# First layer of a two-layer graph network: two edge tiles in one 128 by 384 product, tables of two partial sums, x kept in DRAM

## The chip, the cores and the metric

The kernel runs on one core of a Trainium2 chip. The metric is the device time of one execution in microseconds; the time of a kernel is the median of its runs. A core has five engines that run side by side, each with its own queue of instructions: TensorE (PE; its weight loads are shown as PEld), VectorE (DVE), ScalarE (ACT), GpSimd (POOL) and SyncE (SP), which here issues DMAs. Gathers by index (indirect DMAs) are issued by POOL.

## The reference

12500 nodes with 64 features; 212500 edges, sorted by target node, of which 12500 are self-loops. Each edge has a source, a target, a type out of 16 and 8 attributes.

```python
h = jnp.maximum(_layernorm(x, axis=-1), 0.0)
# layer 0: per edge, the row of its source times the weight of its type; summed by target
for r in range(num_rels):
    mask = etypes == r
    msg = msg + h_src * mask[:, None].astype(feat.dtype) @ weight[r]
x = x + segment_sum(msg, dst)
h = jnp.maximum(_layernorm(x, axis=-1), 0.0)
# layer 1: a small network per edge on (source row, target row, attributes); summed by target
z = jax.nn.relu(concat([h[src], h[dst], edge_attr]) @ W1 + b1)
x = x + segment_sum(z @ W2 + b2, dst)
```

## The kernel before, in words

**Tiles and groups.** Nodes are taken in 98 blocks of 128 rows. The 200000 edges that are not loops are compacted into 1563 tiles of 128 edges, and a group is G = 4 tiles. Since edges are sorted by target, the targets of a tile lie within a window of WT = 12 nodes. The first layer takes the 392 groups of loopless edges (line 1005), the second layer 416 groups of all edges (line 1098).

**The first layer.** For each group POOL gathers the normalised source rows, 128 rows of 64 values per indirect DMA, one per tile (`gather`, line 737), into one of 14 row buffers (`land`, line 303); the first eight groups are gathered from x itself into buffers of their own (32 gathers, `gather_raw`, line 351) and normalised afterwards. ACT makes a one-hot of 16 types by 12 window places for each edge (`relations`, line 750): four ACTIVATEs for the distances and one for the one-hot. PE multiplies, per tile, the rows (128 edges by 64 features) with the one-hot (128 edges by 192) in two halves of HW = 96 columns (`products`, line 983): even types come out on partitions 0 to 63, odd types on 64 to 127. DVE adds the 128 by 96 result into a table at the window of the tile (`add`, line 993). Two tables alternate, each with 8 rows (RH) of 384 nodes: a block pair of 256 nodes and AHEAD = 128 nodes of the next.

**Closing a step.** A step is two blocks, about eight groups. When its groups are added (FIN1, line 139), ACT copies the head of the next step's nodes into the other table (`go_on`, line 771), and `finish` (line 776) folds the table: four pairs of products with `wrel` (line 786), summed in PSUM, then a transposing product; DVE adds the block of x, which lies in SBUF for the whole run (`x_sb`, line 218); then the norm and the projections of the second layer, stored to `a_rows`, `a_early` and `b_rows` by SP. `begin` (line 852) starts the table two steps ahead with the self-loops: PE turns the rows, DVE writes eight rows of the table (line 880).

**What sets the order.** Each engine's instructions are kept in the order in which they are written (`InOrder`, line 316). The work of a step is cut into small pieces by `yield`, and one or more pieces of `open_step` (finish), `fresh` (begin) and `coming` (preparing later edges: compaction, codes, loops) are taken after each add (lines 1048 to 1051). In iteration `it` POOL gathers group it + 8, ACT makes its one-hot, PE multiplies group it + 6 (`L1_PE`, lag 2) and DVE adds group it + 3 (`L1_ADD`, lag 5); near the end the lags shrink to 1 and 2. Products wait in four PSUM buffers of one group (line 1039). The compaction's results are scattered to DRAM by indirect DMAs on POOL, between the gathers (`store`, line 534).

**The second layer.** POOL gathers `a_rows` by source; the first four groups (EARLY) read `a_early`, which misses the last two blocks, and the rest read `a_rows`, after its last store. SP fetches a window of `b_rows` per group (line 1116). PE, DVE and ACT make the hidden rows, PE sums them by target, DVE adds to `sums`; `results` (line 1069) multiplies by W2, adds x from `x_sb` and stores the output.

Of the kernel before, what the change touches and what calls it, by code (L numbers as in the profile page):

```python
# [50 lines left out]
P = 128  # L51
# [20 lines left out]
G = 4  # L72
# [4 lines left out]
HW = RH * WT  # L77
# [31 lines left out]
L1_PE, L1_ADD = (2, 1), (5, 2)  # L109
# [84 lines left out]
def gnn_kernel(  # L194
# [11 lines left out]
    b_rows = dram.tile([NW, D], F32, name="b_rows")  # L206
    dst_l = dram.tile([NGR, G * P], BF16, name="dst_l")
# [10 lines left out]
    x_sb = keep.tile([P, NB * D], F32, name="x_sb")  # L218
    x3 = x_sb.rearrange("p (b d) -> p b d", d=D)
    tail = N - (NB - 1) * P  # L220

    def load_x(b0, Q):

        full = min(b0 + LB, NB - 1)
        Q.dma_start(x3[:, b0:full, :], x[b0 * P : full * P].rearrange("(b p) d -> p b d", p=P))
        if b0 + LB == NB:
            V.memset(x3[:, NB - 1, :], 0.0)
            Q.dma_start(x3[:tail, NB - 1, :], x[(NB - 1) * P :])
# [26 lines left out]
    def layer_norm(pool, b0, nb, name):  # L255

        shape = [P, nb, D]
        mv, rs = stats(pool, x3[:, b0 : b0 + nb, :], nb, name)
        h = pool.tile(shape, F32, name=f"{name}_h")
        V.tensor_tensor(h, x3[:, b0 : b0 + nb, :], bc(mv[:, :, 0], 2, D, shape), op=ALU.subtract)  # L260
        V.scalar_tensor_tensor(h, h, 0.0, bc(rs, 2, D, shape), op0=ALU.max, op1=ALU.mult)
        return h
# [37 lines left out]
    def in_order():  # L300
        with ExitStack() as c2:
# [63 lines left out]
            tables = [own.tile([P, RH, SN + AHEAD], F32, name=f"table{k}") for k in range(2)]  # L365
# [3 lines left out]
            G_.iota(rsel, pattern=[[2, RH]], base=0, channel_multiplier=0, allow_small_or_imprecise_dtypes=True)  # L369
            V.tensor_single_scalar(rsel[D:], rsel[D:], 1.0, op=ALU.add)  # L370
# [12 lines left out]
            wrel = own.tile([P, RH, D], F32, name="wrel")  # L383
# [24 lines left out]
            def weights():  # L408
                for k in range(2):
                    Q_.dma_start(wrel[k * D : (k + 1) * D], w_rel[k::2].rearrange("r i o -> i r o"))  # L410
# [136 lines left out]

            def codes_raw():

                f = prep.tile([P, RAWT], I32, name="raw_f", bufs=1)  # L550
                row = prep.tile([1, RAWT], I32, name="raw_r", bufs=1)
                even = prep.tile([P, RAWT], I32, name="raw_e", bufs=1)
                rel = prep.tile([P, RAWT], I32, name="raw_t", bufs=1)
                d = prep.tile([P, RAWT], F32, name="raw_d", bufs=1)
                ok = prep.tile([P, RAWT], F32, name="raw_ok", bufs=1)
                bad = prep.tile([P, RAWT], F32, name="raw_bad", bufs=1)
                Q_.dma_start(f, raw_f.unsqueeze(0).to_broadcast([P, RAWT]))
                Q_.dma_start(row, raw_f.unsqueeze(0))
# [3 lines left out]
                V_.tensor_single_scalar(even, rel, 1, op=ALU.bitwise_and)  # L562
# [3 lines left out]
                V_.scalar_tensor_tensor(ok, rel, float(R), ok, op0=ALU.is_le, op1=ALU.mult)  # L566
                yield
                V_.tensor_tensor(d, dst_r, f, op=ALU.subtract)
                V_.scalar_tensor_tensor(bad, d, float(WT), d, op0=ALU.is_ge, op1=ALU.mult, accum_out=next(odds_of))
                V_.scalar_tensor_tensor(d, rel, float(WT // 2), d, op0=ALU.mult, op1=ALU.add)  # L570
                yield
                V_.scalar_tensor_tensor(d, even, -float(HW - WT // 2), d, op0=ALU.mult, op1=ALU.add)
                V_.scalar_tensor_tensor(d, d, float(1 + HW - WT), ok, op0=ALU.add, op1=ALU.mult)
# [97 lines left out]
            def codes(c, q, row, psA, V, S, T, rest):  # L671
# [20 lines left out]
                V.tensor_single_scalar(even, rel, 1, op=ALU.bitwise_and)  # L692
                yield
                V.tensor_tensor(d, q[:n, :, :, 1], bc(first_d, 2, P, [n, 2, P]), op=ALU.subtract)
# [5 lines left out]
                V.scalar_tensor_tensor(d, rel, float(WT // 2), d, op0=ALU.mult, op1=ALU.add)  # L700
                V.scalar_tensor_tensor(d, even, -float(HW - WT // 2), d, op0=ALU.mult, op1=ALU.add)
                yield
                V.tensor_single_scalar(ok, rel, 1.0, op=ALU.is_ge)
                V.scalar_tensor_tensor(ok, rel, float(R), ok, op0=ALU.is_le, op1=ALU.mult)
# [4 lines left out]
                V.scalar_tensor_tensor(d, d, float(1 + HW - WT), ok, op0=ALU.add, op1=ALU.mult)  # L709
# [66 lines left out]
            def finish(k, psA):  # L776
# [3 lines left out]
                long = nb == BS  # L780
                if long:
                    yield from rest(2)
# [3 lines left out]
                for r in range(0, RH, 2):  # L786
                    for k in range(2):
# [5 lines left out]
                            stop=(r + 2 == RH),  # L793
                        )
                    if long:
                        yield from rest(2)
# [7 lines left out]
                x_b = x3[:, b0 : b0 + nb, :]  # L804
                V_.tensor_tensor(x_b, x_b, pT[:, :nb, :], op=ALU.add)
                st = wk.tile([P, nb, 6], F32, name="s_st")
# [3 lines left out]
                for i in range(nb):  # L810
                    V_.bn_stats(st[:, i, :], x3[:, b0 + i, :])
# [46 lines left out]
            def some(t, at, b0, n, psA):  # L858
# [20 lines left out]
                yield from rest(2)  # L879
                for r in range(RH):  # L880
# [79 lines left out]
            def first_layer(psA, loops_0):  # L960
# [22 lines left out]
                def products(g, i):  # L983
                    for half in range(2):
                        T_.matmul(
                            pa_of[g][half * D : (half + 1) * D, i, :],
                            lhsT=rows_of[g][:, i, :],
                            rhs=oh_of[g][:, i, half * HW : (half + 1) * HW],
                            start=True,
                            stop=True,  # L990
                        )

                def add(a, i):
                    k = a * G + i
                    if i < n_of[a]:
# [5 lines left out]
                        to = tables[STEP1[a] % 2][:, :, bass.ds(at.pop(k), WT)]  # L1001
                        V_.tensor_tensor(to, to, pa_of[a][:, i, :].rearrange("p (r n) -> p r n", r=RH), op=ALU.add)

                at = {}
                for it in range(NG1 - RAWG + L1_ADD[1]):
                    g = it + RAWG
                    if g < NG1:
# [6 lines left out]
                        if it % 56 == 4 and it // 56 < NB // LB:  # L1014
                            load_x(it // 56 * LB, Q_)
# [21 lines left out]
                    for g in now:  # L1037

                        pa_of[g] = psA.tile([P, G, HW], F32, name="pa", bufs=4)
# [28 lines left out]

            def results(k, ps):
                (b0, nb), t = BLOCKS[k], sums[k % 2]  # L1070
                po = ps.tile([P, BS, D], F32, name="po", bufs=1)
# [5 lines left out]
                V_.tensor_tensor(o[:, :nb, :], po[:, :nb, :], x3[:, b0 : b0 + nb, :], op=ALU.add)  # L1077
# [12 lines left out]
            def second_layer(ps):  # L1090
# [6 lines left out]
                of_z, of_hid, of_pe, of_add = (turns(lag, NGR) for lag in (L2_Z, L2_HID, L2_PE, L2_ADD))  # L1097
                for it in range(NGR + L2_ADD[1]):
# [119 lines left out]
    def in_any_order():  # L1218
        for b0 in range(0, NB, XB):
            load_x(b0, nc.sync)  # L1220
        with ExitStack() as c0:
            rel_rows = dram.tile([NB * P, R * D], F32, name="rel_rows")
# [8 lines left out]
            with ExitStack() as c1:  # L1231
# [114 lines left out]
                def relation_products(b):  # L1346
                    if b % LB == 0:
                        hs[b // LB] = layer_norm(wk, b, LB, "r")
# [163 lines left out]
            with ExitStack() as c3:  # L1512
# [3 lines left out]
                for b0 in range(0, NB, LB):  # L1516
                    h = layer_norm(wk, b0, LB, "s")
# [165 lines left out]
```

## Time and profile before

| | us |
|---|---|
| median of 3 runs | 4092.42 |
| lowest and highest run | 4087.24, 4093.86 |
| the profiled execution | 4087.75 |
| its span, first to last instruction | 4085.9 |
| POOL busy in the span | 3083.5 |
| PE busy | 2422.0 |
| ACT busy | 1640.5 |
| DVE busy | 1146.0 |

A busy time counts the time in which at least one instruction of the engine runs. A line of a group gives the line of the code (here mostly the helper at line 325, so that tiles are told apart by name), the engine, the operation, the tiles written and read, shapes and number; then busy time, mean duration in ns, and the idle time before these instructions with what ended it. "issue" is idle time in which the engine waited for nothing that the profile shows. A line of the order of time begins with the start and the duration in us. The granted clock of PE is given in tenths of full speed.

The gathers from x start at 5.64 us, those from `h_rows` run from 50.9 us to 2002 us, and the second layer's from 2002.35 us to 4075.

### The profile page before, as it was taken

Reading aid. Unit: us, or ns where it says so; the run is one execution under the profiler, and the core shown is the slowest. Engines: PE = TensorE matmul, PEld = TensorE weight load, DVE = VectorE, ACT = ScalarE, POOL = GpSimd, SP = SyncE. Lnnn points to the kernel's source line nnn. Section 1 sums busy time; section 2 is a strip of 40 time slices with the busy share of each in tenths; the row PEclk is TensorE's granted clock in tenths of the full one; section 3 lists DMA queues with packets and bytes.
Section 4 is the critical chain, followed back from the end, with each engine's and each line's share of the span. In section 5 each row is a group of like instructions: output and inputs, shape, how many; then the busy total and the mean of one; then the engine's idle time right before and its main releaser. Section 6 shows DMA issues by size and latency. Waiting matters only on the chain. (4 is left out here: it accounts for less than half of the span.)

```text
span 4085.9 us, 49975 instructions
## 1 busy us (share of the span) xinstructions
PE 2422.0 (59%) x14840; PEld 1853.3 (45%) x14840; DVE 1146.0 (28%) x4671; ACT 1640.5 (40%) x3222; POOL 3083.5 (75%) x3274
## 2 busy tenths in 40 slices
PE   1655655555555555556686666666666666666655
PEld 0433333333333333333475555555555555555555
DVE  7533334333333333333211111111111111111111
ACT  6754545454545454545333222322232222322222
POOL 7777777777777777777777777777777777777776
PEclk9655555555555555555555555555555555555555
DMA  4222222121222222121222121111111112111111
GB/s 124 48 44 64 42 48 44 40 46 40 51 40 45 42 45 42 38 41 37 48 46 42 42 42 44 42 42 42 42 42 42 42 41 44 41 42 42 42 39 36
DMA packets 233554, 184.50 MB, mean 45 GB/s; under 512 B 162969, under 2 KB 171680, under 8 KB 232336
## 3 DMA queue, kind: packets, MB, share of 16 engines
q0 software_dynamic: 104320, 107.70, 14.1%
q1 hardware_dynamic: 115655, 70.30, 6.5%
q10 hardware_dynamic: 13298, 3.20, 0.4%
q8 instruction: 121, 1.98, 0.2%
q14 instruction: 160, 1.31, 0.1%
HBM read 162.74 MB, written 18.20 MB: 44 GB/s over the span
## 5 line engine op out<-in xcount | busy, mean ns | idle before, releaser
L325 POOL DMA_INDIRECT rows<-a_rows,src_i x1645 | 1552.2, 944 | 501.4 <-issue 428.9
L325 POOL DMA_INDIRECT rows<-h_rows,src_c x1535 | 1456.9, 949 | 468.2 <-issue 390.4
L325 PE MATMUL pa<-oh_r,rows 128*64 128x96 f32 x6140 | 836.2, 381 | 780.8 <-DMA rows<-h_rows,src_c 701.9
L325 PE MATMUL pz<-b_win,of_edges 48*128 48x64 f32 x3322 | 819.0, 424 | 686.3 <-ACT of_edges L325 682.1
L325 PEld LDWEIGHTS pz<-b_win,of_edges 48*128 48x128 f32 x3322 | 739.3, 324 | 735.7 <-ACT of_edges L325 712.0
L325 PEld LDWEIGHTS pa<-oh_r,rows 128*64 128x64 f32 x6140 | 472.4, 204 | 1193.8 <-DMA rows<-h_rows,src_c 848.8
L325 ACT ACTIVATE hid<-z 128x256 f32<-128x256 f32 x416 | 172.9, 416 | 1429.7 <-DVE z L325 1399.3
L325 DVE TENSOR_TENSOR z<-pz,rows 128x256 f32<-128x256 f32 x416 | 176.3, 424 | 1652.4 <-DMA rows<-a_rows,src_i 1520.3
L325 ACT ACTIVATE off_r<-iota_s,code 128x192 bf16<-128x192 f32 x1535 | 568.1, 441 | 0.0
L325 DVE TENSOR_TENSOR table<-table,pa 128x96 f32 x1567 | 395.6, 252 | 368.6 <-PE pa L325 262.1
L325 PE MATMUL pa<-oh,hid 128*65 128x40 f32 x3322 | 456.8, 312 | 38.3 <-ACT hid L325 27.2
L325 PEld LDWEIGHTS pa<-oh,hid 128*65 128x65 f32 x3322 | 395.9, 226 | 88.6 <-ACT hid L325 30.8
L325 ACT ACTIVATE oh_r<-off_r 128x768 f32<-128x768 bf16 x392 | 330.2, 842 | 211.5 <-PE pa L325 203.6
L325 DVE SCALAR_TENSOR_TENSOR table<-b_rel,rsel,hT 128x256 f32<-128x256 f32 (+1 forms) x400 | 171.6, 467 | 401.8 <-PE hT L325 391.6
L325 ACT ACTIVATE off<-local_bc,neg_w 40x1024 bf16<-40x1024 bf16 x208 | 235.8, 1134 | 21.5 <-DMA local_bc<-dst_l 12.9
L325 ACT ACTIVATE of_edges<-off 40x1024 f32<-40x1024 bf16 x208 | 219.7, 1056 | 6.5
L325 PE MATMUL pT<-table,wrel 128*64 128x256 f32 (+1 forms) x800 | 200.0, 596 | 2.1 <-DVE table L325 2.1
L325 DVE TENSOR_TENSOR oh<-local,iota_p 128x160 f32<-128x160 f32 x416 | 128.5, 310 | 0.0
L325 DVE TENSOR_TENSOR x_sb<-x_sb,pT 128x128 f32<-128x128 f32 (+1 forms) x50 | 14.2, 284 | 394.5 <-PE pT L325 394.5
L325 ACT COPY table<-table 128x1024 f32<-128x1024 f32 x49 | 51.2, 1045 | 143.0 <-DVE table L325 143.0
L325 ACT ACTIVATE s_rs<-s_mv,eps 128x2 f32<-128x2 f32 (+1 forms) x50 | 14.8, 296 | 230.9 <-DVE s_mv L325 230.9
L325 DVE TENSOR_TENSOR sums<-sums,pa 65x40 f32 x416 | 75.2, 181 | 46.1 <-PE pa L325 33.8
(193 smaller groups left out, 1049.6 us busy)
## 6 DMA issues: line engine op xcount, KB each, us to landing
rows<-a_rows,src_i POOLq DMA_INDIRECT x1645
rows<-h_rows,src_c POOLq DMA_INDIRECT x1535
local_bc<-dst_l SPq DMA_DIRECT2D x104, 160.0 KB
of_edges<-in_attr_t SPq DMA_DIRECT2D x104, 64.0 KB
b_win<-b_rows SPq DMA_DIRECT2D x416, 10.0 KB
b_rel<-t_loop SPq DMA_DIRECT2D x48, 128.0 KB
l_in<-in_rows_l SPq DMA_DIRECT2D x4, 1009.5 KB
b_h<-h_rows SPq DMA_DIRECT2D x48, 64.0 KB
```

Source lines behind the costliest of these rows:

```text
L325: last_ins[self.engine] = getattr(self.engine, name)(*args, **kw)
```

## The change

Two tiles share one product. The rows of tiles i and i + 1 (128 edges by 2 x 64) are multiplied with the one-hots of both (128 edges by 2 x 192). Of the 128 by 384 result the two diagonal blocks are wanted: tile i on partitions 0 to 63, tile i + 1 on partitions 64 to 127. Each is added, 64 partitions by 192, to its half of the table. The table now has 16 rows of types on both halves, and each half is a partial sum; on the lower half types are turned by 8 (`turned_by`), so that the self-loops, which `begin` writes, still need only eight rows, and ACT zeroes the other eight. Folding takes 8 pairs of products instead of 4, and the head copy is twice as wide. PSUM holds two groups instead of four, and the adds follow at lag 3 instead of 5. To make room in SBUF, x isn't kept there: `finish` loads its block of x from DRAM and stores the sum to `x_mid`, and `results` reads that back, loaded two steps ahead.

```diff
-L1_PE, L1_ADD = (2, 1), (5, 2)
+L1_PE, L1_ADD = (2, 1), (3, 2)
...
+    x_mid = dram.tile([NB * P, D], F32, name="x_mid")
...
-    x_sb = keep.tile([P, NB * D], F32, name="x_sb")
...
-            tables = [own.tile([P, RH, SN + AHEAD], F32, name=f"table{k}") for k in range(2)]
+            tables = [own.tile([P, R, SN + AHEAD], F32, name=f"table{k}") for k in range(2)]
...
-            wrel = own.tile([P, RH, D], F32, name="wrel")
+            wrel = own.tile([P, R, D], F32, name="wrel")
+            nought = own.tile([P, 1], F32, name="nought")
...
+            def turned_by(rel, past, V):
+
+                V.tensor_scalar(past, rel, float(RH + 1), -float(R), op0=ALU.is_ge, op1=ALU.mult)
+                V.scalar_tensor_tensor(rel, past, float(RH), rel, op0=ALU.add, op1=ALU.add)
...
+                x_b = wk.tile([P, BS, D], F32, name="x_b", bufs=2)[:, :nb]
...
+                    Q_.dma_start(x_b, x[rows].rearrange("(b p) d -> p b d", p=P))
                 if long:
                     yield from rest(2)
...
-                for r in range(0, RH, 2):
+                for r in range(0, R, 2):
...
                     if long:
-                        yield from rest(2)
+                        yield
...
                 V_.tensor_tensor(x_b, x_b, pT[:, :nb, :], op=ALU.add)
+                Q_.dma_start(x_mid[rows, :].rearrange("(b p) d -> p b d", p=P), x_b)
...
+                for r in range(RH, R, 4):
+                    S_.copy(t[:, r : r + 4, at : at + n * P], bc(nought.to_broadcast([P, n * P]), 1, 4, [P, 4, n * P]))
+                    yield
                 for r in range(RH):
...
                 def products(g, i):
-                    for half in range(2):
-                        T_.matmul(
-                            pa_of[g][half * D : (half + 1) * D, i, :],
-                            lhsT=rows_of[g][:, i, :],
-                            rhs=oh_of[g][:, i, half * HW : (half + 1) * HW],
-                            start=True,
-                            stop=True,
-                        )
+                    if i % 2:
+                        return
+                    n = min(2, n_of[g] - i)
+                    T_.matmul(
+                        pa_of[g][: n * D, i // 2, : n * RW],
+                        lhsT=rows_of[g][:, i : i + n, :].rearrange("p i d -> p (i d)"),
+                        rhs=oh_of[g][:, i : i + n, :].rearrange("p i c -> p (i c)"),
+                        start=True,
+                        stop=True,
+                    )
...
-                        to = tables[STEP1[a] % 2][:, :, bass.ds(at.pop(k), WT)]
-                        V_.tensor_tensor(to, to, pa_of[a][:, i, :].rearrange("p (r n) -> p r n", r=RH), op=ALU.add)
+                        half = slice(i % 2 * D, i % 2 * D + D)
+                        to = tables[STEP1[a] % 2][half, :, bass.ds(at.pop(k), WT)]
+                        V_.tensor_tensor(to, to, pa_of[a][half, i // 2, i % 2 * RW :][:, :RW].rearrange("p (r n) -> p r n", r=R), op=ALU.add)
...
-                        if it % 56 == 4 and it // 56 < NB // LB:
-                            load_x(it // 56 * LB, Q_)
...
-                        pa_of[g] = psA.tile([P, G, HW], F32, name="pa", bufs=4)
+                        pa_of[g] = psA.tile([P, G // 2, 512], F32, name="pa", bufs=2)
...
+            def load_mid(k):
+                b0, nb = BLOCKS[k]
+                mids[k] = wk2.tile([P, BS, D], F32, name="x_r", bufs=3)[:, :nb]
+                Q_.dma_start(mids[k], x_mid[b0 * P : (b0 + nb) * P, :].rearrange("(b p) d -> p b d", p=P))
...
-                V_.tensor_tensor(o[:, :nb, :], po[:, :nb, :], x3[:, b0 : b0 + nb, :], op=ALU.add)
+                V_.tensor_tensor(o[:, :nb, :], po[:, :nb, :], mids.pop(k), op=ALU.add)
```

The path for edges in any order (not taken on these inputs) gets its own copy of x in SBUF.

More of the change, by code (lines that the diff above doesn't have):

```diff
@@ L76 @@
 RH = R // 2
-HW = RH * WT
 AHEAD = 128
@@ L217, in gnn_kernel @@
     V.memset(eps, EPS)
-    x_sb = keep.tile([P, NB * D], F32, name="x_sb")
-    x3 = x_sb.rearrange("p (b d) -> p b d", d=D)
     tail = N - (NB - 1) * P
[L222 to L228, printed above, removed]
     flag = keep.tile([1, 1], I32, name="flag")
@@ L253, in stats, with layer_norm @@
         return mv, rs[:, 1, :]
-    def layer_norm(pool, b0, nb, name):
+    def layer_norm(pool, x3, b0, nb, name):
         shape = [P, nb, D]
@@ L364, in in_order @@
             xf = load_front(fr)
-            tables = [own.tile([P, RH, SN + AHEAD], F32, name=f"table{k}") for k in range(2)]
+            tables = [own.tile([P, R, SN + AHEAD], F32, name=f"table{k}") for k in range(2)]
             src_c = own.tile([P, UPTO[-1]], I32, name="src_c")
             rsel = own.tile([P, RH], F32, name="rsel")
-            G_.iota(rsel, pattern=[[2, RH]], base=0, channel_multiplier=0, allow_small_or_imprecise_dtypes=True)
-            V.tensor_single_scalar(rsel[D:], rsel[D:], 1.0, op=ALU.add)
+            G_.iota(rsel, pattern=[[1, RH]], base=0, channel_multiplier=0, allow_small_or_imprecise_dtypes=True)
+            V.tensor_single_scalar(rsel[D:], rsel[D:], float(RH), op=ALU.add)
             place_c = own.tile([P // 2, PARTS, 2], F32, name="place_c")
@@ L382, in in_order @@
             G_.memset(none, -1.0)
-            wrel = own.tile([P, RH, D], F32, name="wrel")
+            wrel = own.tile([P, R, D], F32, name="wrel")
+            nought = own.tile([P, 1], F32, name="nought")
+            V.memset(nought, 0.0)
             local = own.tile([P, NT], F32, name="local")
@@ L409, in weights @@
                 for k in range(2):
-                    Q_.dma_start(wrel[k * D : (k + 1) * D], w_rel[k::2].rearrange("r i o -> i r o"))
+                    Q_.dma_start(wrel[k * D : (k + 1) * D, :RH], w_rel[k * RH :][:RH].rearrange("r i o -> i r o"))
+                    Q_.dma_start(wrel[k * D : (k + 1) * D, RH:], w_rel[RH - k * RH :][:RH].rearrange("r i o -> i r o"))
                     Q_.dma_start(w1ab[k * D : (k + 1) * D], w1[: 2 * D].rearrange("(k i) o -> i k o", k=2))
@@ L561, in codes_raw @@
                 V_.tensor_single_scalar(rel, rel, float(R + 1), op=ALU.min)
-                V_.tensor_single_scalar(even, rel, 1, op=ALU.bitwise_and)
                 yield
@@ L566, in codes_raw @@
                 V_.scalar_tensor_tensor(ok, rel, float(R), ok, op0=ALU.is_le, op1=ALU.mult)
+                turned_by(rel[:, 1::2], even[:, 1::2], V_)
                 yield
@@ L569, in codes_raw @@
                 V_.scalar_tensor_tensor(bad, d, float(WT), d, op0=ALU.is_ge, op1=ALU.mult, accum_out=next(odds_of))
-                V_.scalar_tensor_tensor(d, rel, float(WT // 2), d, op0=ALU.mult, op1=ALU.add)
+                V_.scalar_tensor_tensor(d, rel, float(WT), d, op0=ALU.mult, op1=ALU.add)
                 yield
-                V_.scalar_tensor_tensor(d, even, -float(HW - WT // 2), d, op0=ALU.mult, op1=ALU.add)
-                V_.scalar_tensor_tensor(d, d, float(1 + HW - WT), ok, op0=ALU.add, op1=ALU.mult)
+                V_.scalar_tensor_tensor(d, d, float(1 - WT), ok, op0=ALU.add, op1=ALU.mult)
                 V_.tensor_scalar(raw_code, d, -1.0, 1.0, op0=ALU.mult, op1=ALU.add)
@@ L691, in codes @@
                 V.tensor_single_scalar(sf, low, float(N - 1), op=ALU.min)
-                V.tensor_single_scalar(even, rel, 1, op=ALU.bitwise_and)
+                V.tensor_single_scalar(ok, rel, 1.0, op=ALU.is_ge)
+                V.scalar_tensor_tensor(ok, rel, float(R), ok, op0=ALU.is_le, op1=ALU.mult)
                 yield
+                turned_by(rel[:, 1], even[:, 1], V)
                 V.tensor_tensor(d, q[:n, :, :, 1], bc(first_d, 2, P, [n, 2, P]), op=ALU.subtract)
@@ L697, in codes @@
                 yield
[L700 to L704, printed above, removed]
+                V.scalar_tensor_tensor(d, rel, float(WT), d, op0=ALU.mult, op1=ALU.add)
                 yield
@@ L708, in codes @@
                     V.scalar_tensor_tensor(ok, place_w, float(RAWE), ok, op0=ALU.is_ge, op1=ALU.mult)
-                V.scalar_tensor_tensor(d, d, float(1 + HW - WT), ok, op0=ALU.add, op1=ALU.mult)
+                V.scalar_tensor_tensor(d, d, float(1 - WT), ok, op0=ALU.add, op1=ALU.mult)
                 V.tensor_scalar(d, d, -1.0, 1.0, op0=ALU.mult, op1=ALU.add)
@@ L780, in finish @@
                 long = nb == BS
+                x_b = wk.tile([P, BS, D], F32, name="x_b", bufs=2)[:, :nb]
+                rows = slice(b0 * P, (b0 + nb) * P)
+                if b0 == NB - 1:
+                    V_.memset(x_b, 0.0)
+                    Q_.dma_start(x_b[:tail, 0], x[b0 * P :])
+                else:
+                    Q_.dma_start(x_b, x[rows].rearrange("(b p) d -> p b d", p=P))
                 if long:
@@ L792, in finish @@
                             start=(r == 0),
-                            stop=(r + 2 == RH),
+                            stop=(r + 2 == R),
                         )
                     if long:
-                        yield from rest(2)
+                        yield
                 yield from rest(2)
@@ L803, in finish @@
                 yield from rest(2)
-                x_b = x3[:, b0 : b0 + nb, :]
                 V_.tensor_tensor(x_b, x_b, pT[:, :nb, :], op=ALU.add)
+                Q_.dma_start(x_mid[rows, :].rearrange("(b p) d -> p b d", p=P), x_b)
                 st = wk.tile([P, nb, 6], F32, name="s_st")
@@ L810, in finish @@
                 for i in range(nb):
-                    V_.bn_stats(st[:, i, :], x3[:, b0 + i, :])
+                    V_.bn_stats(st[:, i, :], x_b[:, i, :])
                 for i in range(nb):
@@ L1066, in first_layer @@
                     pass
+            mids = {}
+            def load_mid(k):
+                b0, nb = BLOCKS[k]
+                mids[k] = wk2.tile([P, BS, D], F32, name="x_r", bufs=3)[:, :nb]
+                Q_.dma_start(mids[k], x_mid[b0 * P : (b0 + nb) * P, :].rearrange("(b p) d -> p b d", p=P))
             def results(k, ps):
                 (b0, nb), t = BLOCKS[k], sums[k % 2]
+                if k + 2 < NFIN:
+                    load_mid(k + 2)
                 po = ps.tile([P, BS, D], F32, name="po", bufs=1)
@@ L1097, in second_layer @@
                 of_z, of_hid, of_pe, of_add = (turns(lag, NGR) for lag in (L2_Z, L2_HID, L2_PE, L2_ADD))
+                for k in range(2):
+                    load_mid(k)
                 for it in range(NGR + L2_ADD[1]):
@@ L1218, in in_any_order @@
     def in_any_order():
-        for b0 in range(0, NB, XB):
-            load_x(b0, nc.sync)
         with ExitStack() as c0:
+            x_sb = c0.enter_context(tc.tile_pool(name="x", bufs=1)).tile([P, NB * D], F32, name="x_sb")
+            x3 = x_sb.rearrange("p (b d) -> p b d", d=D)
+            for b0 in range(0, NB, XB):
+                full = min(b0 + XB, NB - 1)
+                nc.sync.dma_start(x3[:, b0:full, :], x[b0 * P : full * P].rearrange("(b p) d -> p b d", p=P))
+            V.memset(x3[:, NB - 1, :], 0.0)
+            nc.sync.dma_start(x3[:tail, NB - 1, :], x[(NB - 1) * P :])
             rel_rows = dram.tile([NB * P, R * D], F32, name="rel_rows")
@@ L1347, in relation_products @@
                     if b % LB == 0:
-                        hs[b // LB] = layer_norm(wk, b, LB, "r")
+                        hs[b // LB] = layer_norm(wk, x3, b, LB, "r")
                     h = hs[b // LB]
@@ L1516, in in_any_order @@
                 for b0 in range(0, NB, LB):
-                    h = layer_norm(wk, b0, LB, "s")
+                    h = layer_norm(wk, x3, b0, LB, "s")
                     a_st = wk.tile([P, LB, D], F32, name="a_st")
```

## Prediction

> **What bounds the kernel now.** I read the head of the page first, then the costliest groups of POOL, then who waits for whom on POOL, then the order of time at two places.
>
> The head of the page:
>
> ```profile
> span 4085.9 us, 49975 instructions
> PE 2422.0 (59%) x14840; PEld 1853.3 (45%) x14840; DVE 1146.0 (28%) x4671; ACT 1640.5 (40%) x3222; POOL 3083.5 (75%) x3274
> POOL 7777777777777777777777777777777777777776
> PEclk9655555555555555555555555555555555555555
> ```
>
> POOL is at the same seven tenths in every slice, through both layers. The groups of POOL show why (mean ns of one, then the idle time before it):
>
> ```profile
> L325 POOL DMA_INDIRECT rows<-a_rows,src_i x1645 | 1552.2, 944 | 501.4 <-issue 428.9 <-DMA rows<-a_rows,src_i 70.7 <-PE pz L325 0.6
> L325 POOL DMA_INDIRECT rows<-h_rows,src_c x1535 | 1456.9, 949 | 468.2 <-issue 390.4 <-DMA rows<-h_rows,src_c 75.0 <-DVE l_few L325 0.7
> ```
>
> One gather costs 0.944 us and an idle 501.4/1645 = 0.305 us, 1.249 us in all; the first layer's cost 0.949 + 0.305 = 1.254. The list of waits says that this gap isn't a wait for anybody (last column: the longest):
>
> ```profile
> POOL rows L325 <- issue: 823.5, 2702, 0.3
> POOL rows L325 <- DMA rows<-h_rows,src_c: 75.0, 246, 0.3
> POOL rows L325 <- DVE l_few L325: 0.7, 1, 0.7
> ```
>
> No gap is longer than 0.3 us but one, and that one lasts 0.7. POOL issues 3252 indirect DMAs back to back from 5.6 us to 4075: 3252 x 1.25 = 4065 of 4085.9 us. The chain of waits on the page, all of it a 10 us tail behind the last gather, says nothing else. So a change moves the time only by **the number of gathers, their pitch, or a stall of POOL**. The number stays. What is left is to find where POOL could be made to wait, and how far each place is from it now.
>
> **The change, part by part.** The sum is made against the profiled execution: 4087.75 us, of which 1.85 lie outside the span.
>
> *Products.* Eight groups of four tiles take POOL 8 x 4 x 1.25 = 40.0 us. In the window 200 to 1900 us PE is busy 981.3 of 1700 us, so 23.1 in 40. Of these the products are 836.2/1567 tiles = 0.534 x 32 = 17.1, the folding of a block with wrel 196.1/48 = 4.1, the rest 1.9. Afterwards there are 16 products of 384 columns. No row has one; the rows around it:
>
> ```profile
> 99.72 1.55 PE L325 MATMUL pa<-oh_r,raw_rows 128*64 128x96 f32 x16 [1.63 <-DVE table L325]
> 2001.65 1.95 PE L325 MATMUL pT<-table,wrel 128*64 128x128 f32 x16
> 2007.06 0.80 PE L325 MATMUL pab<-w1ab,hT 64*128 64x128 f32 x2 [0.35 <-ACT hT L325]
> 2007.78 1.97 PE L325 MATMUL pT<-table,wrel 128*64 128x128 f32 x16
> ```
>
> Each f32 product is two records, and two column halves run as a pair. A pair costs 1.55/4 = 0.39 us at 96 columns and 1.95/4 = 0.49 at 128, so 0.1/32 = 3.1 ns a column; 384 columns would be 0.49 + 256 x 0.0031 = 1.28. From below, three times a full-width 128-column product back to back (0.40, from four records in 0.80) is 1.2; from above, four times the 96-column pair is 1.55. I take 1.3: 20.8 instead of 17.1. The folding doubles to 8.2. PE then needs 20.8 + 8.2 + 1.9 = 30.9 of 40 us (34.9 by the upper end). It stays under POOL, and POOL has 14 row buffers (70 us of gathers) between itself and PE. Against this speaks the Trainium skill, "TensorEngine Tiling (Array Packing)", Theoretical Speedup: a side of 64 or less can be packed for up to 2x, and the change gives that packing up in the products. By that rule two tiles would cost twice their 0.775, 1.55, and PE would need 34.9: still under 40.
>
> *Adds on DVE.* 1567 adds go from 128x96 (252 ns) to 64 partitions by 192. Between 252 and z's 424 ns at 128x256, 192 elements are 252 + 96 x 1.07 = 355. That is 32 x 0.10 = 3.3 us more per 40, onto 622.5/1700 x 40 = 14.6. The codes lose one pass and gain two over half the elements: nothing.
>
> *ACT.* The head copy of a table doubles (1045 ns to about 2.1 us), and a block gets two zeroing copies of 1024 elements, 2.1 us by the same row: 19.8 + 3.1 = 23 of 40.
>
> *SP.* Eight x loads go; 49 loads, 50 stores and 50 later loads come, at 0.43 us of issue each. None is on POOL's queue. The later loads stand before b_win in SP's queue; SP idled 1484 us there for PE's pz.
>
> So nothing here sets the pitch. A gather is lengthened by something in the first layer: (949 - 944) x 1535 = 7.7 us in all, in a few lumps. One:
>
> ```profile
> 622.06 0.85 DVE L325 SCALAR_TENSOR_TENSOR l_f<-l_f 128x672 f32<-128x672 f32 x1
> 622.26 1.46 POOL L325 DMA_INDIRECT rows<-h_rows,src_c  x1 [0.30 <-issue]
> ```
>
> It began under a long DVE pass from SBUF to SBUF. Such passes stay; the adds, which read PSUM, already run beside 944 ns gathers. I take 0, with both ends at 7.7 us. The skill's "SBUF — State Buffer", Who interferes with whom, says that DVE blocks POOL only in two-port modes or with two SBUF inputs. The new adds have one, so that sum is 0 as well.
>
> **Where POOL could be stalled.** *Start.* The first h_rows gather (50.90) waited 0.4 us beyond the usual gap; at most that is won. ACT gets 5.3 us of zeroing at about 76 us, ahead of the first one-hots. The 15th row group (about 122 us) needs the buffer of the first, whose products ended at 105.2: 17 us of cover, 11 after.
>
> *Stores.* POOL also issues the compaction's scatters, in order, behind DVE. The shortest lead of c_out before its scatter is 15.7 us (1021.4 to 1037.1). PE's two iterations with four folding pairs each become 2.6 + 4 x 1.0 = 6.6 us against 5, so 3 us of lag, and the lag of the adds goes from five groups to three: cover remains.
>
> *Change of layers.* This is the place with the least cover:
>
> ```profile
> 2004.97 0.59 PE L325 MATMUL pa<-oh_r,rows 128*64 128x96 f32 x4 [0.32 <-DMA rows<-h_rows,src_c]
> 2014.65 0.32 SPq L325 DMA_DIRECT2D a_rows<-a_last  x1
> 2015.07 0.38 SPq L325 DMA_DIRECT2D b_rows<-ab  x1
> 2016.68 0.88 SPq L325 DMA_DIRECT2D b_win<-b_rows  x2
> 2022.34 0.94 POOL L325 DMA_INDIRECT rows<-a_rows,src_i  x1 [0.30 <-issue]
> ```
>
> The last a_rows store is issued at 2014.65. The b_win load, which waits for the store issued at 2015.07, starts 1.6 us after it, so a_rows has landed by about 2016.3. POOL wants it at 2022.04, after sixteen a_early gathers: cover 5.7 us. The change lengthens the chain to that store by 1.95 us for each of the two single-block foldings (3.9), 1.05 for the head copy, and up to 3.8 for block 47's four extra pairs, which now push the last three groups' products back; PE's gaps there (0.3 to 0.8 us before each tile) swallow about a third, so 2.5. Together 7.5: a stall of 7.5 - 5.7 = 1.8 us. With all gaps lost and products at 1.55 it is 5; with 3.9 alone it is 0. Behind it the second layer first reads gathered rows at 2031.87 (z), and POOL needs that buffer at 2002.35 + 14 x 5.0 = 2072: covered.
>
> *End.* The x read for the output is fetched two blocks earlier: nothing.
>
> Sum: 4087.75 + 1.8 = about 4090 in the profiled execution. The shown median, 4092.42, lies 4.7 above that execution, so the median forecast is **4094**. Measurement of this kernel can't tell less than 0.2% (8.2 us) from no change.
>
> **Rivals.** *No stall* (0.33): the cover at the change of layers holds, and the time is 4092. For it: five of the 7.5 us are single rows, the rest is scheduling; against: cover and sum are close. *PE becomes the bound* (0.06): if a 384-column product costs over (40 - 8.2 - 1.9)/16 = 1.87 us, PE and not POOL paces the first layer; at 2.0 it needs 42.1, so 2.1 x 48 = 101 us more, 4195. For it: the clock is granted at 0.5, and nothing so wide is in the trace; against: every row gives 1.2 to 1.55. *Stalls beyond the cover* (0.11): scatters or the layer change reach POOL by more than 8 us (14 us more on the chain to a_rows), giving about 4106. *The pitch falls* (0.03): the 7.7 us of long gathers go, with the 0.4 of the start: 4084.
>
> The forecast itself has 0.47. Within 0.2% lie forecast and no stall, 0.80; slower 0.17; faster 0.03. Range: from 4086 (the lowest run, 4087.24, less a little pitch) to 4104 (the highest run, 4093.86, with the 5 us stall and some of the stalls beyond cover); outside are PE as the bound and the far ends.
>
> **What would show it.** Right: POOL's first-layer group at x1535 and 0.30 gaps, 949 ns give or take 4, one wait of some us before the first a_rows gather; 384-column products near 0.65 us a record back to back; PE at 75 to 85% of the first layer. Wrong: POOL gaps over 0.3 us all through the first layer, waiting for PE, or several in front of edges_c.

## The result and the profile after

| | us |
|---|---|
| before, median of 7 runs | 4092.64 (4087.24 to 4093.86) |
| after, median of 7 runs | 4106.63 (4106.42 to 4110.35) |
| after, the profiled execution | 4106.43 |
| its span | 4104.6 |

The ratio of after to before is 1.0036, 95% interval 1.0026 to 1.0046. The changed kernel is 14.0 us slower, and 4106.63 lies above the predicted range (4086 to 4104). The experiments were made in five sessions: in two of them the kernel before took 4088 us, in the other three 5108 to 5144 us (in the traces from there gathers last as long as ever, 943 to 948 ns, but POOL waits long before many of them), and runs of those three are compared only with the kernel before of the same session.

The head of the page of the kernel after:

```profile
span 4104.6 us, 43266 instructions
PE 2653.2 (65%) x10940; PEld 1753.3 (43%) x10940; DVE 1348.5 (33%) x4672; ACT 1774.0 (43%) x3322; POOL 3089.4 (75%) x3274
POOL 7777777777777777777777777777777777777776
PEclk9876667666767676766655555555555555555555
```

POOL is still at seven tenths everywhere, and PE isn't near its limit. At this grain (some 100 us a slice) nothing shows where 14 us went. The costliest groups of POOL, with their idle time, do (kernel after; mean ns, idle time, releasers):

```profile
L315 POOL DMA_INDIRECT rows<-a_rows,src_i x1645 | 1554.9, 945 | 501.5 <-issue 405.2 <-DMA rows<-a_rows,src_i 95.1 <-DVE sums L315 0.9
L315 POOL DMA_INDIRECT rows<-h_rows,src_c x1535 | 1460.1, 951 | 468.5 <-issue 351.2 <-DMA rows<-h_rows,src_c 93.9 <-PE pa L315 12.2
L315 POOL DMA_INDIRECT t_loop<-l_top,l_to x8 | 7.3, 914 | 15.2 <-DVE l_top L315 13.1 <-issue 1.8 <-DVE raw_mv L315 0.3
```

The gathers are almost what they were: 951 ns and 468.5/1535 = 0.305 us of idle time in the first layer, 945 ns in the second (949 and 944 before). Over all gathers the difference adds up to 5.9 us, and with the stall shown below it makes up the 18.7 us between the two profiled spans (the median of before lies 4.9 us above its profiled execution). The longer gathers don't come from the change: late_store below, with all of the added work, has 949 and 944 ns again. The third line is the new thing: of eight scatters one waited 13.1 us for DVE (before, all eight had 2.4 us of idle time). POOL's waits of the kernel after (us in total, times, longest) say that this is the only long one:

```profile
POOL rows L315 <- issue: 760.9, 2496, 0.3
POOL rows L315 <- DMA rows<-h_rows,src_c: 93.9, 308, 0.3
POOL t_loop L315 <- DVE l_top L315: 13.1, 1, 13.1
```

Its place, in POOL's order of time after:

```profile
185.92 0.95 POOL L315 DMA_INDIRECT rows<-h_rows,src_c  x1 [0.30 <-issue]
199.93 0.91 POOL L315 DMA_INDIRECT t_loop<-l_top,l_to  x1 [13.07 <-DVE l_top L315]
201.15 0.96 POOL L315 DMA_INDIRECT rows<-h_rows,src_c  x1 [0.30 <-issue]
```

This is the scatter of the second part of the self-loops' targets. POOL was done with the gather ahead of it at 186.87 and stood until l_top had been written. The 13.07 us hold the usual 0.30, so 12.8 are lost. What DVE did at that time, after:

```profile
175.90 0.15 DVE L315 CAST l_d<-l_in 128x1 f32<-128x1 int32 x1
...
182.41 0.35 DVE L315 TENSOR_TENSOR ab<-pab,b_bc 128x64 f32<-128x64 f32 x2 [4.22 <-ACT ab L315]
...
199.47 0.18 DVE L315 TENSOR_SCALAR l_top<-l_top_i 128x32 f32<-128x32 int32 x1
```

and before:

```profile
163.87 0.15 DVE L325 CAST l_d<-l_in 128x1 f32<-128x1 int32 x1
...
179.58 0.18 DVE L325 TENSOR_SCALAR l_top<-l_top_i 128x32 f32<-128x32 int32 x1
179.71 1.53 DVE L325 TENSOR_TENSOR table<-table,pa 128x96 f32 x5
```

(`l_d` is the first thing that DVE makes of the loaded `l_in`.) So l_top was ready at 179.76 before and at 199.65 after, 19.9 us later: 12.0 of them were there when the work on l_top began (163.87 and 175.90), the rest came on the way. The lateness alone would have been covered: before, POOL came to this scatter at 202.00, after 148 gathers, and after at 186.87, after 136. The **lead** of the data (POOL free, plus the usual 0.30, less data ready) went from 202.00 + 0.30 - 179.76 = +22.5 us to 186.87 + 0.30 - 199.65 = -12.5. The swing of 35.0 us has two parts, **15.1 us of order and 19.9 of a later DVE**. The order shifts because the scatter is one of the pieces that are taken after the adds, in the order written: the adds at lag 3 come two iterations, eight gathers, sooner in POOL's order than at lag 5.

Other scatters lost lead as well and kept enough. That of c_out at 1037 went from 15.7 us to 11.5, that at 543 from 22.3 to 10.2.

### The profile page after: what moved, and what is told of

Its sections match the earlier page's. It is cut to its first block, busy times and chain, and to the rows that moved or that the text cites. A ratio compares the mean times of both kernels' runs of the same rounds, so it can differ in the third digit from the quotient of the medians.

```text
span 4104.6 us, 43266 instructions
## 1 busy us (share of the span) xinstructions
PE 2653.2 (65%) x10940; PEld 1753.3 (43%) x10940; DVE 1348.5 (33%) x4672; ACT 1774.0 (43%) x3322; POOL 3089.4 (75%) x3274
## 5 line engine op out<-in xcount | busy, mean ns | idle before, releaser
L315 POOL DMA_INDIRECT rows<-h_rows,src_c x1535 | 1460.1, 951 | 468.5 <-issue 351.2
L315 PE MATMUL pa<-oh_r,rows 128*128 128x384 f32 x1536 | 982.4, 740 | 576.3 <-DMA rows<-h_rows,src_c 432.9
L315 DVE TENSOR_TENSOR table<-table,pa 64x192 f32 x1567 | 552.2, 352 | 927.1 <-PE pa L315 875.1
L315 PEld LDWEIGHTS pa<-oh_r,rows 128*128 128x128 f32 x1536 | 321.1, 257 | 1084.3 <-issue 769.4
L315 PE MATMUL pT<-table,wrel 128*64 128x256 f32 (+1 forms) x1600 | 249.6, 443 | 0.0
L315 ACT ACTIVATE off<-local_bc,neg_w 40x1024 bf16<-40x1024 bf16 x208 | 235.9, 1134 | 20.3 <-DMA local_bc<-dst_l 10.3
L315 PEld LDWEIGHTS pT<-table,wrel 128*64 128x64 f32 x1600 | 112.7, 158 | 170.7 <-issue 148.5
L315 ACT COPY table<-table 128x2048 f32<-128x2048 f32 x49 | 93.0, 1898 | 44.1 <-DVE table L315 41.4
L315 ACT COPY table<-nought 128x1024 f32<-128x1024 f32 (+1 forms) x100 | 101.8, 1025 | 0.0
```

The costliest lines, as they stand in the source:

```text
L315: last_ins[self.engine] = getattr(self.engine, name)(*args, **kw)
```

## The experiments

The times named in the expectations start from the 4092.64 and 4106.63 us of the result. In the two sessions at 4088 us the kernel before took 4.7 and 5.0 us less, so such a time has to be lowered by about 5 us before a measured one is held against it.

Theory: the whole 14 us are this one stall, made of order and late DVE together. Rivals: the pitch of the gathers and PE's added work cost it all through the layer; or DVE is late because of one added piece of work (ACT's zero copies, SP's x_mid store ahead of a load, the longer adds, the folding), or because two PSUM buffers hold the products back.

This table sums up the sessions at 4088 us, with the two traces of the result. The first three columns are read from the order of time of POOL and DVE; the last is against the kernel before of the same session (half_adds_c and half_fold_c are single runs).

| kernel | gathers ahead of the scatter | POOL free | l_top ready | POOL waited | time over before |
|---|---|---|---|---|---|
| before | 148 | 202.00 | 179.76 | 0.3 | 0 |
| lag3_c | 140 | 192.16 | 179.90 | 0.3 | 0.0 |
| lag3_two_c | 140 | 190.63 | 184.61 | 0.3 | -1.6 |
| late_store | 152 | 207.25 | 202.47 | 0.3 | +0.7 |
| half_adds_c | 136 | 186.80 | 194.95 | 8.4 | +8.4 |
| half_fold_c | 136 | 186.32 | 199.12 | 13.1 | +12.7 |
| no_zeros | 136 | 186.20 | 199.00 | 13.1 | +14.1 |
| after | 136 | 186.87 | 199.65 | 13.1 | +14.0 |
| x_mid_last | 136 | 186.52 | 200.57 | 14.3 | +12.8 |
| early_store | 132 | 181.29 | 200.72 | 19.7 | +20.3 |

The last two columns agree within 2 us in every row: **what POOL waits there is what the kernel pays.**

### late_store: the scatter later in the order

```diff
-            def loops(q, rows, pauses=(8, 16)):
+            def loops(q, rows, pauses=(24, 16)):
```

The first number is how many empty pieces stand between l_top and its scatter.

> The changed kernel with one number altered: in the later three parts of the loops the first scatter on POOL stands 24 pieces behind the DVE work that fills it instead of 8, so 16 pieces, four groups or about 16 gathers (20 us) later in POOL's order. In the changed kernel's trace POOL was free for the second part's scatter at 186.87 us and its data were ready 12.5 us after that. Theory 'one stall' (the time lost is that one wait): the wait goes and the time falls by about 12.8 us, to 4093 to 4095, no different from before by more than 0.1%. Rival 'broad loss' (the first layer is slower as a whole, through longer gathers and a later change of layers, and the wait only shows it at one place): the wait goes from this place, POOL waits elsewhere or its gathers stay long, and the time stays above 4101.

Measured: 4088.32 us in 11 runs against 4087.60 in 17, ratio 1.0002 (0.9993 to 1.0011). POOL's order of time in late_store:

```profile
206.31 0.94 POOL L315 DMA_INDIRECT rows<-h_rows,src_c  x1 [0.30 <-DMA rows<-h_rows,src_c]
207.56 0.91 POOL L315 DMA_INDIRECT t_loop<-l_top,l_to  x1 [0.30 <-DVE table L315]
```

DVE is as late as in the changed kernel (202.47), but POOL comes to the scatter behind 152 gathers, at 207.25, and doesn't wait. All the rest of the change is in this kernel, and it takes the time of the kernel before. So the stall is shown to be the cost, within the 4 us or so that the interval leaves, and the rival of the pitch and of PE's work falls. It doesn't beat the kernel before either.

### early_store: the scatter sooner

```diff
-            def loops(q, rows, pauses=(8, 16)):
+            def loops(q, rows, pauses=(0, 16)):
```

> The opposite of the run before: the scatter stands 0 pieces behind its data instead of 8, so two groups or 8 gathers (10 us) earlier in POOL's order. Theory 'one stall': the wait at the second part grows by about 10 us, to 23, and the later two parts, whose data lead POOL by 11.1 and 11.0 us in the changed kernel, come to a lead near 1, so nothing or a few us more: 4116 to 4121 in all. Rival 'broad loss': the place of the scatter decides little, and the time moves by less than 4 us.

Measured: 4107.94 us, ratio 1.0053 (1.0037 to 1.0068), 20.3 us over before. POOL in early_store:

```profile
201.01 0.91 POOL L315 DMA_INDIRECT t_loop<-l_top,l_to  x1 [19.72 <-DVE l_top L315]
```

The wait grows with the order, as the theory has it, by 6.7 us (5.6 of order, 1.1 of a later l_top) and not by 10: eight pieces were four gathers here, not eight. So the time falls short of the 4116 to 4121 expected, also when these are lowered by 5. The later two parts didn't stall.

### x_mid_last and no_zeros: SP's queue and ACT's zeroing

The load of l_in, from which l_top is made, was issued at 143.13 us before and at 170.26 after, right behind the new x_mid store. x_mid_last puts that store behind the others of the block:

```diff
-                Q_.dma_start(x_mid[rows, :].rearrange("(b p) d -> p b d", p=P), x_b)
...
-                for t, to in [(a, a_early)] * (b0 < NB - 2) + [(a, a_rows), (ab[:, 1, :nb, :], b_rows)]:
+                for t, to in [(a, a_early)] * (b0 < NB - 2) + [(a, a_rows), (ab[:, 1, :nb, :], b_rows), (x_b, x_mid)]:
```

> The changed kernel with the store of x_mid moved behind the stores of a and b on SP. In the changed kernel SP issued the load of the second loops part (l_in) at 170.26 us, right behind an x_mid store that had waited for DVE; in the kernel before it was issued at 143.13. Theory 'SP's queue' (DVE is late because its input comes late): l_in is issued 10 to 25 us earlier, DVE writes l_top some 10 us earlier, and most of the 13 us wait of POOL goes: about 4095 to 4098. Theory 'pace of the catching up' (DVE reaches that work late whatever is loaded, since DVE had no idle time in front of its first use of l_in): l_in is issued earlier, the wait stays within 2 us of 13, and the time within 2 us of 4106.6.

Measured: 4100.41 us, ratio 1.0035 (1.0022 to 1.0048). The load is now issued at 158.83, 11 us sooner, and l_top is not sooner at all (200.57). SP's queue isn't the cause; DVE came late to data that lay ready. The time, too, is the one that the second theory expected (4106.6 lowered by 5, within 2).

no_zeros leaves out ACT's zeroing copies after the first three steps, with their places in the order kept, so the table holds old sums:

```diff
+                    if len(zeroed) < 6:
+                        zeroed.append(r)
+                        S_.copy(t[:, r : r + 4, at : at + n * P], bc(nought.to_broadcast([P, n * P]), 1, 4, [P, 4, n * P]))
```

> The changed kernel with ACT's zeroing of the upper eight table rows left out after the first three calls, the pieces kept in place (so the partial sums hold old values: the output is not the reference's). It takes 2.1 us a step from ACT. Theory 'ACT paces the catching up': two steps are done before the stall, so l_top comes 4 us or more earlier and the wait falls from 13 to 9 or less, 4102 or less in all. Rival 'PE and DVE pace it' (two PSUM buffers tie each product to the adds two groups earlier): the wait changes by less than 2 us, and the time stays at 4105 to 4107.

Measured: 4101.74 us, ratio 1.0035 (1.0022 to 1.0049), the same wait of 13.07 us, l_top at 199.00. In the kernel after, four of the copies left out stand between 151 and 184 us, 4.2 us in all. They are not the cause; of those of the first three steps this says nothing.

### lag3 and lag3_two: the shorter lag and the two buffers, in the kernel before

```diff
-L1_PE, L1_ADD = (2, 1), (5, 2)
+L1_PE, L1_ADD = (2, 1), (3, 2)
```

and, in lag3_two alone:

```diff
-                        pa_of[g] = psA.tile([P, G, HW], F32, name="pa", bufs=4)
+                        pa_of[g] = psA.tile([P, G, HW], F32, name="pa", bufs=2)
```

They were first run where the kernel before took 5108 and then 5144 us:

> The kernel before with one number altered: the adds follow three groups behind instead of five, as in the changed kernel; four PSUM buffers and everything else as before. The pieces of the preparation are taken after each add, so POOL's order should move: the scatter of the second loops part should stand about two groups (8 of the 12 gathers by which it stands earlier in the changed kernel) earlier, at 140 gathers instead of 148. Theory 'order plus pace': data as before, near 180 us, lead down from 22.5 to 8 to 13 us, no wait, the time the same as before within 0.1%. Rival 'order alone': the lag brings the wait by itself, and the time rises by over 5 us.

> The run before, and two PSUM buffers for the products instead of four, as in the changed kernel; the old products, adds and folding. Theory 'two buffers pace the catching up' (each product waits for the adds two groups earlier, and DVE's order ties those to ACT): l_top of the second loops part is written 10 us or more later than in the run with the lag alone, the lead falls to about 0 or below, and the time is 0 to 10 us above before. Rival 'wider work paces it' (longer products, adds and copies): l_top comes within 3 us of the run with the lag alone, no wait, the time as before.

Measured: lag3 1.0031 (1.0020 to 1.0043) and, repeated, 1.0032 (1.0021 to 1.0044); lag3_two 1.0039 (1.0025 to 1.0054) and 1.0051 (1.0032 to 1.0070). In the trace of lag3 from there POOL waited 34.3 us at this scatter (264.06 to 298.33); with DVE so late for another reason, these runs say nothing of the case at 4088 us. Run again there:

> The kernel before with L1_ADD = (3, 2) alone, at the usual time of the kernel before (4088 to 4093). Theory (order and late DVE, the second from the change's work in the catching up, not from the lag): the scatter stands at 140 gathers, POOL is free for it 10 us earlier than before (192 us), l_top is ready near 180 as before, lead about +12, no wait, ratio 1.000. Rival (the lag alone makes DVE late): l_top near 190 to 200, POOL waits 0 to 8 us, ratio up to 1.002.

> As lag3_c with two PSUM buffers for the products in place of four. If two buffers (product g waits for the adds of g-2) make DVE late, l_top comes at 190 to 200 us against lag3_c's 180 and POOL waits up to 8 us, ratio 1.000 to 1.002. If it is the wider adds and the doubled folding, l_top comes within 3 us of lag3_c's and POOL doesn't wait, ratio 1.000.

Measured: lag3_c 4087.96 against 4087.97, ratio 1.0001 (0.9991 to 1.0010); lag3_two_c 4086.35, 0.9997 (0.9988 to 1.0007). POOL in lag3_c:

```profile
191.22 0.94 POOL L325 DMA_INDIRECT rows<-h_rows,src_c  x1 [0.30 <-DMA rows<-h_rows,src_c]
192.47 0.92 POOL L325 DMA_INDIRECT t_loop<-l_top,l_to  x1 [0.30 <-issue]
```

The one line of the lag moves the scatter from 148 to 140 gathers and POOL from 202.00 to 192.16, 9.8 of the 15.1 us of order. l_top stays at 179.90: at this time DVE doesn't follow POOL, it is catching up. Two buffers make l_top 4.7 us later (184.61), between the two forecasts for lag3_two_c (190 to 200, or within 3 us of lag3_c). DVE's waits for products and PE's for adds between 90 and 178 us, that is, before l_top, in lag3_c and then in lag3_two_c:

```profile
DVE table L325 <- PE pa L325: 1.2, 2, 0.6
PE pa L325 <- DVE table L325: 2.6, 2, 1.8
```

```profile
DVE table L325 <- PE pa L325: 7.2, 8, 1.8
PE pa L325 <- DVE table L325: 9.6, 9, 3.1
```

With two buffers product g waits for the adds of g - 2 (7.0 us more), and then DVE waits for the product (6.0 us more). Neither the lag nor the buffers are enough for a stall: a lead of +6.3 us is left.

### half_adds and half_fold: the added work of DVE and of PE

half_adds adds only the first 96 of the 192 columns, eight of the sixteen types (the expectation's "four of the eight" is a miscount of the same cut), and half_fold leaves out four of the eight folding pairs; in both, half of the sums are missing.

```diff
-                        to = tables[STEP1[a] % 2][half, :, bass.ds(at.pop(k), WT)]
-                        V_.tensor_tensor(to, to, pa_of[a][half, i // 2, i % 2 * RW :][:, :RW].rearrange("p (r n) -> p r n", r=R), op=ALU.add)
+                        to = tables[STEP1[a] % 2][half, :RH, bass.ds(at.pop(k), WT)]
+                        V_.tensor_tensor(to, to, pa_of[a][half, i // 2, i % 2 * RW :][:, : RW // 2].rearrange("p (r n) -> p r n", r=RH), op=ALU.add)
```

```diff
-                    for k in range(2):
+                    for k in range(2 if r % 4 == 0 else 0):
```

> The changed kernel with each add over four of the eight types only (64 x 96 in place of 64 x 192), so the tables and the output are not the reference's. If the longer adds are what makes l_top 20 us later, l_top comes near 185 us in place of 199.7 and POOL has no wait there: near 4094. If not, l_top stays within 5 us of 199.7 and the wait within 5 of 13.1: 4102 to 4107.

> The changed kernel with four of the eight folding pairs of a block left out, so that half of the types are missing from the output. If the doubled folding is what makes l_top 20 us later, l_top comes near 185 us and POOL has no wait there: near 4094. If not, l_top stays within 5 us of 199.7 and the wait within 5 of 13.1: 4102 to 4107.

Measured (single runs, the kernel before at 4087.97): half_adds_c 4096.39, half_fold_c 4100.64. POOL's waits in half_adds_c, then in half_fold_c:

```profile
POOL t_loop L315 <- DVE table L315: 8.4, 1, 8.4
```

```profile
POOL t_loop L315 <- DVE l_top L315: 13.1, 1, 13.1
```

The longer adds are worth 199.65 - 194.95 = 4.7 us, a third of the 15 us that the theory of the adds expected: l_top and the wait stay, barely, within the bounds of "if not"; the time lies just under those bounds, lowered by 5. The folding is worth 0.5, which one run can't tell from nothing. Both kernels had also been run twice in the sessions above 5100 us (5181.08 and 5188.98 against 5108.32; 5212.26 and 5209.25 against 5143.66), where they tell nothing of this.

### half_products: PE's longer products

Some 10 of the 19.9 us were left, if the parts found so far may be added. half_products multiplies with the one-hot of the first tile alone (192 columns) and adds both halves from there; half_products_four has four PSUM buffers of half the size as well. The tables are wrong in both.

```diff
-                        pa_of[g][: n * D, i // 2, : n * RW],
+                        pa_of[g][: n * D, i // 2, :RW],
...
-                        rhs=oh_of[g][:, i : i + n, :].rearrange("p i c -> p (i c)"),
+                        rhs=oh_of[g][:, i, :],
```

> The changed kernel with each product over the first tile's 192 columns only, of which both blocks are added, so the tables and the output are not the reference's. PE's products cost about half (0.65 us per two tiles). If the longer products make up the open 10 us, l_top comes near 190 us in place of 199.7 and POOL's wait falls to 2 to 5 us: 4092 to 4097. If they don't, l_top stays within 3 us of 199.7 and the wait at 10 to 13 us: 4100 to 4106.

> As half_products, with four PSUM buffers of half the size in place of two, so that product g no longer waits for the adds of g-2; the adds stay at 64 x 192. If products and buffers together make DVE late, l_top comes at 184 to 187 us (the longer adds' 4.7 are left) and POOL waits 0 to 1 us: 4087 to 4092. If what is left is ACT's (head copies, zero copies) or DVE's alone, l_top stays above 193 and the wait above 6 us: 4096 to 4104.

Measured: 5225.89 and 5195.98 us, against 5139.92 for the kernel before. There, too, everything is late: POOL waited 51 and 49 us at this scatter, and the question that they were made for stays open.

## Why the prediction was wrong

**The step that failed** stands under *Stores*: "the lag of the adds goes from five groups to three: cover remains". Cover didn't remain: POOL stood 12.8 us at one scatter, of `l_top`, which the prediction never names. Three things were wrong in it. It took the place with the shortest lead (c_out, 15.7 us) for the place in danger. What decides is the lead less what the change takes at that very place: 4.2 us at c_out, 35 at l_top, which had 22.5. It counted nothing against the shorter lag; but POOL's scatter is a piece that hangs on the adds, and comes 9.8 us sooner in POOL's order by the lag alone (lag3_c). And it priced DVE, ACT and PE by their share of a steady step of 40 us, while in the first 200 us the engines are catching up with gathers that lie ready. In the kernel before PE waits for a gather ahead of nearly every tile from 160 us on; in the kernel after it doesn't do so once between 90 and 178 us. There, added time in the loop of products, adds and buffers can make the next piece later. The trace of before could have given warning. The 113th add starts at 172.21 us, in the midst of the work on l_top; 112 longer adds of 0.10 us each are at most 11.2 us, and eight gathers sooner 10.0. Together that is 21.2 of the 22.5 us of lead, before buffers or products are counted. (Measured, the adds were worth 4.7 us and the eight gathers 9.8; in the kernel after the 113th add started at 196.12.)

*Stalls beyond the cover* (0.11, "scatters or the layer change reach POOL by more than 8 us", 4106) was what happened, in its first half: a scatter reached POOL. That 4106 is met is luck. It was made of 14 us more on the chain to a_rows, where nothing was paid, and no lead of a scatter went into it.

**What makes DVE 19.9 us late** is settled in part. Two buffers give 4.7 us (shown in the kernel before), longer adds 4.7 (one run); folding, the later zero copies and SP's order give less than 1. Some 10 us are open. Longer products, and the way in which they and the buffers lengthen each other, are argued from DVE's and PE's waits alone; ACT's doubled head copies (1.90 us each, before 1.04) weren't tried. Of the order, 9.8 of 15.1 us are the lag; that the rest comes from the two new pieces of `begin`, which push the pieces of `coming` forward at the end of a step, is read from the code and wasn't tried.

**What held.** POOL's pitch is the bound and didn't change: late_store, with all of the added work, is at 1.0002. No engine became the bound. An add was forecast at 355 ns and took 352. The change of layers:

```profile
2035.91 0.34 SPq L315 DMA_DIRECT2D a_rows<-a_last  x1
```

```profile
2037.35 0.94 POOL L315 DMA_INDIRECT rows<-a_early,src_i  x1 [0.30 <-issue]
2038.60 0.94 POOL L315 DMA_INDIRECT rows<-a_rows,src_i  x1 [0.30 <-issue]
```

From the first a_early gather (2018.58 after, 2002.35 before) the last store of a_rows comes 17.33 us later, before 12.30: the chain grew by 5.0 us, not 7.5. Of the cover of 5.7 some 0.7 is left, and there is no stall. So the forecast's 1.8 us, the one term of its sum, weren't paid either; *no stall* was right for this place.

**Right for a wrong reason** was the product of 384 columns. Forecast 1.3 us per two tiles; its group after (records, busy time) gives 981.9/767 = 1.28, at two records each:

```profile
L315 PE MATMUL pa<-oh_r,rows 128*128 128x384 f32 x1534 | 981.9, 740 | 576.3 <-DMA rows<-h_rows,src_c 432.9 <-DVE table L315 75.0 <-issue 33.0
```

Yet it isn't one duration but two. PE in the order of time after, and then busy times and clock of two stretches (the third number from the end is PEclk):

```profile
304.17 0.88 PE L315 MATMUL pa<-oh_r,rows 128*128 128x384 f32 x2 [0.60 <-DMA rows<-h_rows,src_c]
...
320.72 1.62 PE L315 MATMUL pa<-oh_r,rows 128*128 128x384 f32 x2 [1.17 <-DMA rows<-h_rows,src_c]
```

```profile
317.00:333.00 16.00, 10.39 (x18) 3.82 (x16) 5.88 (x20) 8.17 (x18) 12.04 (x14) 0.50 0.17 37
300.00:314.00 14.00, 8.72 (x43) 3.43 (x42) 4.23 (x12) 8.15 (x18) 10.53 (x12) 1.00 0.14 31
```

At a granted clock of 0.50 a lone product of two records takes 1.62 us, above the prediction's upper end of 1.55, and at 1.00 it takes 0.88. The prediction read its rows without asking which clock they stood at. All four rows of its part on products stood at 0.50, and the row ahead of the first, with the same sixteen records, stood at 1.00 (before):

```profile
97.21 0.88 PE L325 MATMUL pa<-oh_r,raw_rows 128*64 128x96 f32 x16 [0.87 <-DVE table L325]
```

At 0.50, then, 1.3 was too low: two products back to back took 2.90 us, 1.45 each. The mean came out at 1.28 because with the change the clock was higher: between 200 and 1900 us it is 0.70 on average, before 0.52 (lag3_c 0.52, late_store 0.69). That pays for the wider products and also makes folding cheaper (242.5 us in all, where twice the 196.1 of before were forecast), so that PE is busy 1180 of these 1700 us, 69% and not 77%.

The Trainium skill's "TensorEngine Tiling (Array Packing)", Theoretical Speedup, gives packing up to 2x for a side of 64 or less. By that rule two tiles would take twice the packed 0.775 us, 1.55 as an estimate. The 0.775 and the 1.45 measured here both stood at a clock of 0.50, so packing was worth 1.9x, which agrees. It would make nothing of the time, since PE isn't the bound.

## What to carry to other kernels

For each instruction that an in-order bottleneck engine issues on another engine's data, list lead **at its own place**, and take off both what the change adds to the data and what it takes from the order: a shorter lag moves every piece that hangs on it, also the scatter on the busiest queue. Price a catching-up phase by itself; a share of 70% in the steady state says nothing of it. And when the cost is one stall of a known scatter, moving that scatter in the order is the repair: sixteen empty pieces gave back the 14 us, to within the noise.

## What the runs showed of the hardware

PE's granted clock was higher with the change: 0.70 on average from 200 to 1900 us with 16 products of 128 by 384 per eight groups, 0.52 with 64 half-width products of 96 columns, for 69% and 58% of the time busy. Most of the rise goes with the products: with four of the eight folding pairs left out (half_fold_c, one run) it is still 0.65. In the stretches looked at it is 0.50 or 1.00 with mixtures between, and a product takes 1.62 or 0.88 us. The share of busy time doesn't tell the two apart: in the rows above PE was busy 10.39 of 16 us at 0.50, with no gap over 1.9 us between its instructions, and 8.72 of 14 us at 1.00.

The Trainium skill's "TensorE: Matmul & The Clock Gate", Part 1: The HAM clock gate, has two states, at half and at full rate, by how busy PE has been; the two durations agree with two states. How busy the array must be for the full clock, no run here was made to tell.
